# v's rows by plain fp32 products instead of split products and transposes, and eight new constants for the planner

## The chip, the cores and the metric

The kernel runs on one core of one Trainium2 chip. The metric is the device time of one execution in microseconds (us); the kernel before took 1351.64 us, the median of three executions (1351.54, 1351.64 and 1353.74 us). Five engines work side by side, each on its own instruction queue in order: TensorE (PE), VectorE (DVE), ScalarE (ACT), GpSimd (POOL) and SyncE (SP, which here only issues DMAs).

## The reference

The input x has 8 sequences of 512 rows and 128 channels, in fp32. Four residual blocks follow each other, each on the layer-normalised rows:

1. a Mamba-like block: input projection, depthwise convolution with silu, a scan over time with 8 states per channel, output projection;
2. a mixture of experts: 8 experts with hidden width 512, each `silu(x @ w_gate) * (x @ w_up)` and then `@ w_down`, weighted per row by a router;
3. attention with 16 heads of 8 channels, in which a row sees its own chunk of 10 rows and 25 rows to the left;
4. the same mixture of experts again.

In the attention block, `q = x @ Wq.T + bq`, and likewise k and v, where x is the normalised row. The scores are softmaxed under the mask and multiplied with v, and Wo follows. The change touches only how v is computed, and the constants of the planner.

## The kernel before

**The stream.** The experts are the spine of the program. For 2 passes of 8 sequences, 8 experts and 4 quarters of the hidden width there are three products on PE: g, u and y (128x128 weights against 512 columns). Each is a sum of three fp32r products, since weights and inputs are split into a high and a low part (`matmul3`, L489). Between them ACT computes silu(g), DVE multiplies by u, ACT or DVE rounds to the high part h0, and POOL subtracts to get the low part h1 (`hidden`, L1246). There are 2 x 8 x 8 x 4 = 512 such quarters. Only the first four experts of the first sequence are done in halves of 256 columns. The stream of a quarter needs a free PSUM bank for g, one for u, and h0 and h1 some quarters later for y.

**The side work.** Everything else (Mamba fronts and backs, router preparations, attention) is written as Python generators, "lanes", that yield the engine they need next. A planner written in the kernel (`Clock` L129, `Lanes` L280) keeps an own estimate of when each engine is free and decides, in Python and before the program is compiled, where in the stream's order each piece of side work goes. So the order of the instructions on each engine is fixed at build time; on the chip, semaphores alone decide when each starts. The planner's constants are at L94 to L120. The change touches these:

- `LATE` (L97, used at L1067): how early the router's exponentials may be placed when the wrong activation table is loaded;
- `SIDE` (L98) and `JOIN_MAX`, `JOIN_END` (L101, L103; `start`, L320): how long a side product that is ready waits so as to stand beside other side products;
- `WARM_GAP`, `WARM_TO` (L108, L109; `keep_warm`, L1763): where the planner expects PE to idle for longer than the gap, up to this place in the stream, it puts in a product whose result nobody uses (tile `idle`);
- `PRESS` and `HELD` (L111, L112; `tick`, L335): how much a late lane may push, and how long a lane is held back while the stream waits.

All instructions go through the wrapper at L269, so nearly every line of the profile says L269; groups are told apart by the names of tiles. Table loads of ACT that the kernel asks for itself are at L569.

**Attention's preparation.** `attention_consts` (L1328) runs once. `attention_prep` (L1341) runs once per sequence. It loads the rows, normalises them (`normalised`, L542; four PE transposes into `tp_a`, then high and low parts `axt`), and makes q and k by `matmul3` into `aqk`. Their pieces `apc` go to DRAM (`aqd`). Then, for v:

- three fp32r products of 512 columns give v transposed (`avp`); ACT adds the bias, one value per partition (`avf`);
- four PE transposes of 128x128 bring it back to rows (`avt`); ACT copies it to `avs`;
- one DMA of 256 KB writes `avs` to DRAM (`avd`), from where the attention's steps load windows of rows (`avr`).

`avf`, `avs` and the working tile `arest` of q and k share one buffer (tag "rest", one copy). The tile `xn` of a normalisation has one buffer too (`LNB = 1`), given back once its last reader is placed.

Of the kernel before, what the change touches and what calls it, by code (L numbers as in the profile page):

```python
# [8 lines left out]
F32 = mybir.dt.float32  # L9
# [3 lines left out]
AF = mybir.ActivationFunctionType  # L13
ALU = mybir.AluOpType
# [4 lines left out]
P = 128  # L19
B, L, DIM = 8, 512, 128  # L20
NT = L // P
# [47 lines left out]
B_BV = B_ROUTE + 32  # L69
# [24 lines left out]
AHEAD = 0.2  # L94
EDGE = 0.1
FIRST = 0.6
LATE = 0.3  # L97
SIDE = 0.5  # L98
JOIN = 2.0
JOIN_DUE = 0.0  # L100
JOIN_MAX = 6.0  # L101
JOIN_ATT = 3.0
JOIN_END = 2.0  # L103
MOST = 6
OTHERS = 4
AT_FIRST = 7
WARM = 3.5
WARM_GAP = 0.25  # L108
WARM_TO = 1.5  # L109
SECOND = 0.2  # L110
PRESS = 0.4  # L111
HELD = 0.18  # L112
MAMBA_DUE = 0.9
PREP_DUE = 0.9
ATT_LEAD = 2.5
# [164 lines left out]
class Lanes:  # L280
# [39 lines left out]
    def start(self, lane):  # L320
# [5 lines left out]
        if need == "T":  # L326
            if lane in self.urgent:
                return c.now if c.based("T", ready) <= c.now else INF
            wait = SIDE
            if not c.beside and not self.starved:  # L330
# [4 lines left out]
    def tick(self):  # L335
# [3 lines left out]
        while True:  # L339
            c.now = max(c.now, c.end["T"])  # L340
            first, best = c.now + AHEAD, None
            for lanes in (self.urgent, self.lanes):
                for lane in lanes:
# [3 lines left out]
                    else:  # L347
                        edge = PRESS if lane[4] and lane[4]() else 0.0
                        if self.starved:
                            edge = -HELD  # L350
                    if s <= c.now + max(AHEAD, edge) and s - edge < first:
# [26 lines left out]
def block_kernel(ctx: ExitStack, tc: tile.TileContext, x, pack_a, pack_b, pack_c, w_qkv, mask, mask_t, w_o,  # L378
# [3 lines left out]
    lanes = Lanes(clock)  # L382
    pe = Engine(nc.tensor, "T", clock)
    act = Engine(nc.scalar, "A", clock)
    dve = Engine(nc.vector, "V", clock)
    pool = Engine(nc.gpsimd, "P", clock)
    sp = Engine(nc.sync, "S", clock)

    const = ctx.enter_context(tc.tile_pool(name="const", bufs=1))
    dram = ctx.enter_context(tc.tile_pool(name="dram", bufs=1, space=DRAM))  # L390
    lnp = ctx.enter_context(tc.tile_pool(name="lnp", bufs=LNB))
    fp = ctx.enter_context(tc.tile_pool(name="fp", bufs=2))
    qp = ctx.enter_context(tc.tile_pool(name="qp", bufs=1))
# [32 lines left out]
    def sides(*tiles):  # L426
        while not bank("others", OTHERS if "first" in done else AT_FIRST, len(tiles)):
            yield lambda: bank("others", OTHERS if "first" in done else AT_FIRST, len(tiles))
        return take("others", *zip(*tiles))

    def side(shape, name):
        return (yield from sides((shape, name)))[0]

    def freed(t, who="others"):

        held[who] -= 1
        lanes.give("bank", t + TO_PE)
        return t
# [36 lines left out]
    pb = const.tile([P, B_COLS], F32, name="pb")  # L475

    ident = const.tile([P, P], F32, name="ident")
# [11 lines left out]
    def matmul3(dst, w, v, start=True, stop=True, after=0.0):  # L489

        clock.beside = False
        pe.matmul(dst, w[0], v[0], start=start, stop=False, after=after)
        pe.matmul(dst, w[1], v[0], start=False, stop=False)
        return pe.matmul(dst, w[0], v[1], start=False, stop=stop)
# [47 lines left out]
    def normalised(xc, tag, halves, nt=NT, give=True, quick=False, plain=False):  # L542


        yield "V", xc[1]
        xn = yield from layernorm(xc, tag, nt, quick)
        if give:
            lanes.give("x", max(clock.end["V"], clock.end["A"]))
        tp = yield from side([P, L], f"tp_{tag}")
        for t in range(nt):  # L550
            e = pe.transpose(tp[:, t * P : (t + 1) * P], xn[:, t, :], ident)
        if not plain:
            lanes.give("ln", e)
        yield "A"
        hi, lo = halves()
        tp = tp[:, : nt * P]
        e = act.copy(hi, tp)
        if plain:
            xn = xn.rearrange("p t d -> p (t d)")[:, : nt * P]
            e = act.copy(xn, tp)  # L560
        yield "V"
        freed(max(e, dve.tensor_tensor(lo, tp, hi.bitcast(F32), ALU.subtract)))
        yield "T"
        return (hi, lo, xn) if plain else (hi, lo)
# [458 lines left out]
    def ffn_prep(k, b, xc, t0=0, nt=NT):  # L1023
# [42 lines left out]

        yield lambda: clock.table in TABLES[AF.Exp] or pos[0] >= k * B + b - LATE  # L1067
        yield "A"
# [43 lines left out]
    def ffn_finish(k, b, acc):  # L1112
        xo, there = yield from load_x(b, 2 * k + 1, f"fo{k}_{b}")
        yield "T", there
        tp = yield from side([P, NT, DIM], f"yp{k}_{b}")
        for t in range(NT):
            pe.transpose(tp[:, t, :], acc[:, t * P : (t + 1) * P], ident)
        yield "V"
        freed(dve.tensor_tensor(xo, xo, tp, ALU.add))
        yield "S"  # L1120
        store_x(b, 2 * k + 2, xo)

    def ffn_stream():
# [14 lines left out]
        def weighted(k, b, e, cs, y, there):  # L1138
# [25 lines left out]
            elif left[0] == 0:  # L1164
                lanes.add(ffn_finish(k, b, state.pop(("acc", k, b))), rank=FRANK, ready=t, joins=JOIN_END)

# [161 lines left out]
    def attention_consts():  # L1328
        raw = qp.tile([P, 3, P], F32, tag="rest", name="wqkv")
        there = sp.dma_start(out=raw, in_=w_qkv) + 1.5  # L1330
        yield "A", there
        consts = []
        for i, nm in enumerate(("wq", "wk", "wv")):
            consts.append((yield from split_const(raw[:, i, :], P, nm)))
            yield "A"
        return consts

    scaling = HD ** -0.5
# [2 lines left out]
    def attention_prep(b, consts):  # L1341
        xc = yield from load_x(b, 2, f"a{b}")

        def halves():
            return [qp.tile([P, L], F32R, tag=f"t{i}", name=f"axt{b}_{i}") for i in range(2)]

        xt = yield from normalised(xc, f"a{b}", halves)
        stacks = []
        for m, (bcol, order) in enumerate(((B_BQ, Q_PIECES), (B_BK, K_PIECES))):
            pp = yield from side([P, L], f"aqk{b}_{m}")  # L1350
            matmul3(pp, consts[m], xt)
            yield "A"

            bias = pb[:, bcol : bcol + 1]

            qd = dram.tile([2, len(order), P // 2, L], BF16, tag=f"qd{m}", name=f"aqd{b}_{m}", bufs=2)

            def put(piece, pi):
                js = [j for j, o in enumerate(order) if o == pi]
                places = slice(js[0], js[-1] + 1, js[1] - js[0] if len(js) > 1 else 1)  # L1360
                for s in range(2):
                    half = piece[64 * s : 64 * s + 64, None, :]
                    sp.dma_start(
                        out=qd[s, places].rearrange("j r t -> r j t"),
                        in_=half.to_broadcast([64, len(js), L]),
                    )

            ps_ = [qp.tile([P, L], BF16, tag="pc", name=f"apc{b}_{m}_{i}", bufs=3) for i in range(3)]
            rest = qp.tile([P, L], F32, tag="rest", name=f"arest{b}_{m}")
            act.activation(ps_[0], pp, AF.Identity, bias=bias)  # L1370
            yield "V"
            freed(dve.scalar_tensor_tensor(rest, pp, bias, ps_[0], ALU.add, ALU.subtract))
            put(ps_[0], 0)
            yield "V"
            dve.tensor_copy(ps_[1], rest)
            yield "V"
            dve.tensor_tensor(ps_[2], rest, ps_[1], ALU.subtract)
            put(ps_[1], 1)
            yield "S"
            put(ps_[2], 2)  # L1380
            stacks.append(qd.rearrange("s j (d p) t -> s (j d) p t", p=NPAIR))
            yield "T"
        vp = yield from side([P, L], f"avp{b}")
        matmul3(vp, consts[2], xt)
        yield "A"
        vf = qp.tile([P, L], F32, tag="rest", name=f"avf{b}")
        freed(act.activation(vf, vp, AF.Identity, bias=pb[:, B_BV : B_BV + 1]))
        yield "T"
        vt = yield from side([P, NT, P], f"avt{b}")
        for t in range(NT):  # L1390
            pe.transpose(vt[:, t, :], vf[:, t * P : (t + 1) * P], ident)
        yield "A"
        vs = qp.tile([P, NT, P], F32, tag="rest", name=f"avs{b}")
        freed(act.copy(vs, vt))
        yield "S"
        vd = dram.tile([L, P], F32, tag="vd", name=f"avd{b}", bufs=2)
        e = sp.dma_start(out=vd.rearrange("(t p) d -> p t d", p=P), in_=vs)
        heads[b] = stacks[0], stacks[1], vd, e + 3.0

    def attention_preps():  # L1400
# [19 lines left out]
    def attention(sb):  # L1420
# [62 lines left out]
        def scores(s, both):  # L1483

            qs, ks, _ = loaded[s]
            for m in range(NPAIR):
                for h in range(2):
                    rows = slice(64 * h, 64 * h + QROWS)
                    for i, (q, k) in enumerate(blocks(steps[s][1])):
# [4 lines left out]
                        )  # L1494
            lanes.add(maxima(s, both, e), joins=JOIN_MAX)

# [101 lines left out]
        def outputs(s, o, e):  # L1598
# [11 lines left out]
            if t == len(QTILES) - 1:  # L1610
                lanes.add(joined(b, outs.pop(b)), rank=JRANK, ready=e, joins=JOIN_END)

# [103 lines left out]
    with mctx:  # L1716
# [28 lines left out]
        while (0, 0) not in ready or ready[0, 0][1] == 0:  # L1745
            if lanes.tick():
                continue
            if clock.now > WARM:
                sel = mc["sel"]
                e = pe.matmul(warm[:, :HALF], sel[:, 0], sel[:, : HALF // P], start=True, stop=True)  # L1750
# [12 lines left out]
        def keep_warm():  # L1763

            if pos[0] < WARM_TO and clock.now > clock.end["T"] + WARM_GAP and lanes.are_free("bank"):
                t, = take("experts", [[P, L]], ["idle"])
# [94 lines left out]
```

## Time and profile before

| what | value |
|---|---|
| median of three executions | 1351.64 us |
| the profiled execution | 1351.62 us |
| its span, first to last instruction | 1349.8 us |
| PE busy | 1328.9 us, 98% of the span |
| DVE, ACT, POOL busy | 1036.8, 964.7, 940.4 us |
| DMA queue for data, share of 16 engines | 33.9% |
| v's products `avp` (24 of them) and transposes `avt` (32) | 9.6 us and 5.1 us busy |
| ACT's `avf` and `avs`, one per sequence each | 686 and 586 ns median |
| mean granted clock of PE | 0.996 |

A time of PE's instructions is given in two ways. The duration of one matmul includes the latency through the array (393 ns for 512 columns), and the matmuls overlap; what counts for the end is the time from the start of one to the start of the next. In the timeline, that is the difference of the start times of two rows. "Idle before" names what an engine waited for.

### The profile page before, as it was taken

How to read it: one execution, taken by the hardware profiler on the slowest of the kernel's cores; microseconds unless marked ns; L12 is line 12 of the kernel's file. 1: busy time of each engine (PE TensorE's matmuls, PEld its weight loads, DVE VectorE, ACT ScalarE, POOL GpSimd, SP SyncE). 2: the span in 40 equal slices, each digit the busy share in tenths (PEclk: the TensorE clock that was granted, in tenths of full speed). 3: DMA queues.
4: the chain of work that ended last, by engine and by line, in shares of the span. 5: the costliest groups of instructions: out<-in, count | busy, mean ns of one | idle time of the engine just before them, and what ended most of it. 6: DMA issues, size and time to landing. Idle time of an engine off the chain costs nothing.

```text
span 1349.8 us, 29533 instructions
## 1 busy us (share of the span) xinstructions
PE 1328.9 (98%) x10261; PEld 1053.3 (78%) x10261; DVE 1036.8 (77%) x3114; ACT 964.7 (71%) x1694; POOL 940.4 (70%) x1042
## 2 busy tenths in 40 slices
PE   7999999999999999999999999999999999999998
PEld 7877778788788877777777777777777777778887
DVE  6887888688888867898788887888888787855443
ACT  7768576867787556777777777777877767765654
POOL 5877576776767757666766767767677676777776
PEclk9999999999999999999999999999999999999999
DMA  3321304232112242344345444454544434222111
GB/s 126 95 72 38 87 24 101 62 81 73 45 48 56 63 85 54 73 97 118 79 103 111 99 106 100 104 109 89 118 91 104 119 71 88 61 69 55 40 40 40
DMA packets 230861, 107.75 MB, mean 80 GB/s; under 512 B 86417, under 2 KB 226616, under 8 KB 230712
## 3 DMA queue, kind: packets, MB, share of 16 engines
q1 hardware_dynamic: 230712, 105.87, 33.9%
q8 instruction: 81, 1.33, 0.4%
q14 instruction: 68, 0.56, 0.1%
HBM read 77.64 MB, written 27.79 MB: 78 GB/s over the span
## 4 chain that ended last, share of the span: by engine, by line
PE 89%; POOL 3%; ACT 3%; issue 3%; DVE 2%; DMA 0%; POOLq 0%; DVEq 0%
PE u L269 25%; PE y L269 25%; PE g L269 25%; PE ao L269 2%; PE aw L269 2%; PE as L269 2%; POOL h L269 1%; PE mo L269 1%; PE aqk L269 1%; ACT h L269 1%; DVE h L269 1%; PE mde L269 1%; PE aout L269 1%; PE yp L269 1%; ACT L269 1%
## 5 line engine op out<-in xcount | busy, mean ns | idle before, releaser
L269 POOL TENSOR_TENSOR h<-h,h 128x512 fp32r<-128x512 f32 x492 | 640.0, 1310 | 279.0 <-ACT h L269 219.4
L269 PE MATMUL u<-xt_f,wu 128*128 128x512 f32 (+1 forms) x1584 | 451.5, 395 | 3.5 <-ACT h L269 2.7
L269 PE MATMUL g<-xt_f,wg 128*128 128x512 f32 (+1 forms) x1584 | 448.3, 393 | 2.1 <-ACT h L269 1.9
L269 PE MATMUL y<-h,wd 128*128 128x512 f32 (+1 forms) x1584 | 445.5, 392 | 1.4 <-POOL h L269 0.8
L269 DVE TENSOR_TENSOR h<-u,h 128x512 f32<-128x512 f32 x420 | 285.9, 686 | 157.5 <-PE u L269 109.3
L269 ACT ACTIVATE h<-g 128x512 f32<-128x512 f32 x512 | 303.4, 597 | 123.2 <-PE g L269 100.1
L269 ACT CAST h<-h 128x512 fp32r<-128x512 f32 x437 | 268.4, 619 | 171.2 <-DVE h L269 169.6
L269 PEld LDWEIGHTS g<-xt_f,wg 128*128 128x128 f32 x1584 | 288.5, 189 | 70.3 <-ACT h L269 3.0
L269 PEld LDWEIGHTS y<-h,wd 128*128 128x128 f32 x1584 | 288.3, 188 | 70.2 <-POOL h L269 1.4
L269 PEld LDWEIGHTS u<-xt_f,wu 128*128 128x128 f32 x1584 | 286.6, 189 | 71.7 <-ACT h L269 4.1
L269 POOL TENSOR_TENSOR acc<-acc,cwb 128x512 f32<-128x512 f32 (+1 forms) x114 | 148.0, 1298 | 52.5 <-DVE cwb L269 33.8
L269 ACT ACT_TABLE_LOAD x109 | 139.8, 1283 | 24.7 <-PE g L269 23.2
L269 DVE CUSTOM_DVE_ANT_0 amasked<-as,maskq 128x60 f32<-128x60 f32 x640 | 95.4, 213 | 5.0 <-PE as L269 4.8
L269 DVE TENSOR_TENSOR cwb<-y,cwb 128x512 f32<-128x512 f32 (+1 forms) x116 | 77.5, 668 | 16.0 <-PE y L269 14.4
L269 DVE TENSOR_TENSOR apt<-aw,maskk 125x400 f32<-125x400 f32 (+2 forms) x160 | 88.1, 570 | 0.0
L269 DVE SCALAR_TENSOR_TENSOR h<-h,g 128x512 f32<-128x512 f32 x92 | 62.3, 681 | 27.0 <-ACT h L269 26.6
L269 ACT ACTIVATE apt<-apt 125x400 f32<-125x400 f32 (+2 forms) x160 | 81.5, 540 | 0.4
L269 DVE SCALAR_TENSOR_TENSOR h<-u,h 128x512 f32<-128x512 f32 x92 | 62.6, 683 | 3.3 <-PE g L269 0.5
L269 DVE DVE_READ_ACCUMULATOR2_ANT amx<- 128x1 f32 x640 | 52.1, 81 | 0.0
L269 DVE CAST h<-h 128x512 fp32r<-128x512 f32 x75 | 48.8, 651 | 1.2
L269 DVE COPY v<-avr 125x128 f32<-125x128 f32 (+2 forms) x40 | 25.7, 644 | 26.4 <-PE ao L269 26.4
L269 PEld LDWEIGHTS ao<-apt,v 125*32 125x32 f32 (+2 forms) x1280 | 27.4, 109 | 14.6 <-DVE h L269 4.4
(205 smaller groups left out, 1239.5 us busy)
## 6 DMA issues: line engine op xcount, KB each, us to landing
cwb<-cwd_f SPq DMA_DIRECT2D x124, 256.0 KB
aqd<-apc SPq DMA_DIRECT2D x32, 192.0 KB
ks<-aqd SPq DMA_DIRECT2D x48, 93.8 KB
x_fo<-x SPq DMA_DIRECT2D x16, 256.0 KB
aqd<-apc SPq DMA_DIRECT2D x32, 128.0 KB
x_f<-x SPq DMA_DIRECT2D x15, 256.0 KB
qs<-aqd SPq DMA_DIRECT2D x48, 75.0 KB
aod<-aos SPq DMA_DIRECT2D x24, 100.0 KB
```

Of the source, the lines that this page charges most:

```text
L269: f(*args, **kw)
```

## The change

`attention_consts` no longer splits Wv into two parts; it copies it as plain fp32. It also makes a tile `bv` in which every partition holds v's bias along the columns: POOL spreads the bias column over a 128x128 tile (`bvs`), one PE product with the identity turns it (`abv`), and ACT copies it out.

`attention_prep` asks `normalised` for the plain fp32 copy of the transposed rows too (one more ACT copy out of PSUM, `xn_a` from `tp_a`), as the router's preparation does already. Right after the normalisation, v's rows come directly from four fp32 products: the stationary operand is a 128x128 slice of the transposed rows, and the moving one is Wv. DVE adds `bv` while it reads the result from PSUM into `avs`, and the DMA to `avd` follows. q and k come after that. The `xn` buffer of the normalisation is given back after v's products.

The eight constants above get new values, so the planner places the whole program anew.

```diff
-LATE = 0.3
-SIDE = 0.5
+LATE = 0.4
+SIDE = 0.6
-JOIN_MAX = 6.0
+JOIN_MAX = 8.0
-JOIN_END = 2.0
+JOIN_END = 5.0
-WARM_GAP = 0.25
-WARM_TO = 1.5
+WARM_GAP = 0.15
+WARM_TO = 2.5
-PRESS = 0.4
-HELD = 0.18
+PRESS = 0.3
+HELD = 0.1
...
-        for i, nm in enumerate(("wq", "wk", "wv")):
+        for i, nm in enumerate(("wq", "wk")):
             consts.append((yield from split_const(raw[:, i, :], P, nm)))
             yield "A"
+        wv = const.tile([P, P], F32, name="wv")
+        act.copy(wv, raw[:, 2, :])
+
+        wide = qp.tile([P, P], F32, tag="t0", name="bvs")
+        yield "P"
+        pool.tensor_copy(wide, pb[:, B_BV : B_BV + 1].to_broadcast([P, P]))
+        yield "T"
+        bp = yield from side([P, P], "abv")
+        pe.matmul(bp, wide, ident, start=True, stop=True)
+        bv = const.tile([P, P], F32, name="bv")
+        yield "A"
+        freed(act.copy(bv, bp))
+        consts += wv, bv
...
-        xt = yield from normalised(xc, f"a{b}", halves)
+        *xt, xf = yield from normalised(xc, f"a{b}", halves, plain=True)
+        vt = yield from side([P, NT, P], f"avt{b}")
+        for t in range(NT):
+            e = pe.matmul(vt[:, t, :], xf[:, t * P : (t + 1) * P], consts[2], start=True, stop=True)
+        lanes.give("ln", e)
+        yield "V"
+        vs = qp.tile([P, NT, P], F32, tag="rest", name=f"avs{b}")
+        freed(dve.tensor_tensor(vs, vt, consts[3][:, None, :].to_broadcast([P, NT, P]), ALU.add))
+        yield "S"
+        vd = dram.tile([L, P], F32, tag="vd", name=f"avd{b}", bufs=2)
+        v_end = sp.dma_start(out=vd.rearrange("(t p) d -> p t d", p=P), in_=vs)
+        yield "T"
...
-        vp = yield from side([P, L], f"avp{b}")
-        matmul3(vp, consts[2], xt)
-        yield "A"
-        vf = qp.tile([P, L], F32, tag="rest", name=f"avf{b}")
-        freed(act.activation(vf, vp, AF.Identity, bias=pb[:, B_BV : B_BV + 1]))
-        yield "T"
-        vt = yield from side([P, NT, P], f"avt{b}")
-        for t in range(NT):
-            pe.transpose(vt[:, t, :], vf[:, t * P : (t + 1) * P], ident)
-        yield "A"
-        vs = qp.tile([P, NT, P], F32, tag="rest", name=f"avs{b}")
-        freed(act.copy(vs, vt))
-        yield "S"
-        vd = dram.tile([L, P], F32, tag="vd", name=f"avd{b}", bufs=2)
-        e = sp.dma_start(out=vd.rearrange("(t p) d -> p t d", p=P), in_=vs)
```

More of the change, by code (lines that the diff above doesn't have):

```diff
@@ L1362, in put @@
                     half = piece[64 * s : 64 * s + 64, None, :]
-                    sp.dma_start(
+                    end = sp.dma_start(
                         out=qd[s, places].rearrange("j r t -> r j t"),
@@ L1366, in put @@
                     )
+                return end
             ps_ = [qp.tile([P, L], BF16, tag="pc", name=f"apc{b}_{m}_{i}", bufs=3) for i in range(3)]
@@ L1379, in attention_prep @@
             yield "S"
-            put(ps_[2], 2)
+            e = put(ps_[2], 2)
             stacks.append(qd.rearrange("s j (d p) t -> s (j d) p t", p=NPAIR))
             yield "T"
-        vp = yield from side([P, L], f"avp{b}")
-        matmul3(vp, consts[2], xt)
-        yield "A"
-        vf = qp.tile([P, L], F32, tag="rest", name=f"avf{b}")
-        freed(act.activation(vf, vp, AF.Identity, bias=pb[:, B_BV : B_BV + 1]))
-        yield "T"
-        vt = yield from side([P, NT, P], f"avt{b}")
-        for t in range(NT):
-            pe.transpose(vt[:, t, :], vf[:, t * P : (t + 1) * P], ident)
-        yield "A"
-        vs = qp.tile([P, NT, P], F32, tag="rest", name=f"avs{b}")
-        freed(act.copy(vs, vt))
-        yield "S"
-        vd = dram.tile([L, P], F32, tag="vd", name=f"avd{b}", bufs=2)
-        e = sp.dma_start(out=vd.rearrange("(t p) d -> p t d", p=P), in_=vs)
         heads[b] = stacks[0], stacks[1], vd, e + 3.0
```

## The prediction

> **What bounds the kernel now.** I read the page first (busy shares, clock, chain), then PE's list of waits, then PE's timeline around v's work and around each long wait, and ACT's timeline at one of them.
>
> ```profile
> PE 1328.9 (98%) x10261; PEld 1053.3 (78%) x10261; DVE 1036.8 (77%) x3114; ACT 964.7 (71%) x1694; POOL 940.4 (70%) x1042
> ...
> PE 89%; POOL 3%; ACT 3%; issue 3%; DVE 2%; DMA 0%; POOLq 0%; DVEq 0%
> ```
>
> PE is busy 98% of the span, and 89% of the chain that ended last is PE. So a microsecond of start-to-start time on PE is a microsecond of the whole, and work of other engines costs only where it makes PE wait. The next view is PE's timeline around v's work of one sequence (start, duration, instruction).
>
> ```profile
> 608.46 0.50 PE L269 MATMUL avp<-axt,wv_hi 128*128 128x512 f32 x1
> 608.80 0.40 PE L269 MATMUL avp<-axt,wv_lo 128*128 128x512 f32 x1
> 609.03 0.39 PE L269 MATMUL avp<-axt,wv_hi 128*128 128x512 f32 x1
> 609.26 0.86 PE L269 MATMUL y<-h,wd 128*128 128x512 f32 x3
> 609.96 0.86 PE L269 MATMUL g<-xt_f,wg 128*128 128x512 f32 x3
> ...
> 614.17 0.60 PE L269 MATMUL avt<-ident,avf 128*128 128x128 f32 x4
> 614.60 0.22 PE L269 MATMUL amt<-eye,mp 128*80 128x128 bf16 x1
> 614.63 0.94 PE L269 MATMUL g<-xt_f,wg 128*128 128x512 f32 x3
> 615.42 0.87 PE L269 MATMUL u<-xt_f,wu 128*128 128x512 f32 x3
> ```
>
> A stream triple takes 0.70 (609.26 to 609.96). The triple after a small product takes 0.79 (614.63 to 615.42): a switch of shape costs about 0.09. `avp` took 0.80 here, after the attention's `aw`; `avt` took 0.43. Plain fp32 products of the very shape that the change puts in exist already, in the attention's output `aout`:
>
> ```profile
> 1083.77 1.05 PE L269 MATMUL aout<-wo,aat_t 128*128 128x128 f32 x8
> 1084.58 0.95 PE L269 MATMUL g<-xt_f,wg 128*128 128x512 f32 x3
> ```
>
> Four such products take 0.81 between stream triples (eight rows, since an fp32 product runs in two), and 0.91 after `aw` (642.03 to 642.94 in the same view).
>
> PE's other time is waiting. I took each group on PE, start to start, against the median of groups with the same kind and neighbours. The medians sum to 1326.4; 17.9 us lie above them, 2.3 before the first and 3.2 after the last. Of the 17.9, the opening to 33 us holds 2.3, 59 to 92 us 5.9, 122 to 131 us 1.3, 148 to 153 us 1.3, 173 to 182 us 3.75, 262 to 267 us 1.7, 520 us 0.9; nearly nothing comes later. The largest place, on PE, on ACT, and its granted clock (third column from the right):
>
> ```profile
> 173.81 0.86 PE L269 MATMUL y<-h,wd 128*128 128x512 f32 x3
> 176.60 1.64 PE L269 MATMUL g<-xt_f,wg 128*128 128x512 f32 x3 [1.94 <-ACT h L269]
> 178.04 1.48 PE L269 MATMUL u<-xt_f,wu 128*128 128x512 f32 x3
> 179.32 1.19 PE L269 MATMUL y<-h,wd 128*128 128x512 f32 x3
> ...
> 169.68 1.28 ACT L569 ACT_TABLE_LOAD   x1
> 170.97 1.95 ACT L269 ACTIVATE mdec<-mdelta,nega 128x512 f32<-128x512 f32 x3
> ...
> 177.00:181.00 4.00, 4.00 (x18) 0.62 0.12 30
> ```
>
> ACT runs a Mamba batch between two table loads while silu(g) queues behind it; PE runs out of banks, waits 1.94, and then runs at a clock of 0.62 for three triples.
>
> **The change, part by part.**
>
> *v's products on PE.* Gone are 8 triples `avp` (5.76 start to start, all rows) and 8 times 4 `avt` (4.14): 9.9 us. In the changed order v's products stand between stream triples in four sequences, after `aw` in three, and before a small product in one: 4 x 0.81 + 3 x 0.91 + 0.9 = 6.9. Gain 3.0. The bounds per sequence are 0.81 and 1.09 (`aout` between two `aw`), so a gain of 1.2 to 3.4.
>
> *The bias tile.* `abv` is one 128x128 fp32 product, 0.22 by `mo` from `pa`, with a switch of 0.09: +0.3, once. POOL's `bvs` (about 0.2 by the small copies), ACT's copies of `wv` and `bv` (0.28 each, like `win`), less a rounding and a subtraction of the old split: beside the stream.
>
> *Shape switches.* From the order: 450 between the stream, the packed small products and single 128x128 products before, 455 after. By kind (five more back to the stream from single ones, five fewer from packed ones, at 0.08 and 0.10) that is nothing. One more `idle` product: 0.1. **PE's own work: -2.7**, as the same medians put over the changed order also give.
>
> *ACT, DVE, SP.* Per sequence ACT loses `avf` (0.69) and `avs` (0.59) and gains `xn_a` (0.58, as `axt`); DVE gains one add from PSUM (0.68 as `axt`). ACT is 71% and DVE 77% busy, and where PE does not wait the stream covers them: zero, unless they fall into a batch (below). SP's `avd` issue (0.37, 256 KB) now stands ahead of the twelve `aqd` issues of q and k; the readers come hundreds of microseconds later for the first sequences. The normalisation's only buffer is held for 5 to 9 us more per sequence; the order was made with that and places the next normalisation behind it. Cover: the preparations run a whole sequence ahead. If it is gone, the price is a wait like the one at 520 us, 0.9 each.
>
> *The planner's constants: where the waits go.* The first 203 PE instructions (to about 41 us) are the same, and so is the end from the last y of the second expert of the last sequence on. Between them I summed, per quarter of an expert, ACT's rows between two silus against PE's rows of that quarter, and carried on what ACT did not get done. This backlog, in us, against what PE lost:
>
> - before: 7.4 at 59 us (5.9 lost), 4.6 at 116 us (1.3), 5.7 at 167 us (3.75), 5.7 at 257 us (1.7); below 4 nothing.
> - changed order, same places in the stream: 7.0, then 6.2, then 5.1, then 4.1; elsewhere at most 4.2.
>
> So at the third place the batch is 1.2 shorter (the copies `xt_f` and `xn_f` stand elsewhere): the wait of 2.1 falls to about 1.0 and, like the wait of 1.45 at 265.42, should leave the clock alone: -2.7. The fourth goes: -1.7. The second grows by 1.6 of backlog: +1.0 (bounds 0 and 2.5, that of the third). In 59 to 92 us ACT has 0.4 less and 4 `idle` products stand instead of 10, but DVE's backlog by the same count peaks at 10.4 instead of 8.2 and stays 2 to 4 higher: +0.5 (bounds -3 and +3). For waits that appear where I see none: +1.3, one of the small kind (bounds 0 and 3.75). The places at 148 and 520 us: unchanged. Sum of waits: -1.6.
>
> On the price of a wait the Trainium skill ("TensorE: Matmul & The Clock Gate", section on HAM oscillation) gives another rule: no idle gaps on PE above about 3.4 us. By it a 1.94 us gap costs only itself; the rows above show 1.65 more at a clock of 0.62. By the rule the third place would give back 1.1 instead of 2.7, and the sum would be 1348.9.
>
> **Sum.** -2.7 - 1.6 = -4.3. The profiled execution took 1351.62 (span 1349.8 and 1.8 around it), the same as the median 1351.64: **1347.3 us**.
>
> **Rivals.**
>
> *The waits only move.* The batches are the same in number (124 table loads for 125), and a place with less ACT backlog gets more of DVE. For it: DVE's higher count at 64 to 92 us. Against: the two shorter batches. Then the waits stay at 17.9 and PE's own gain is left: 1348.9, or, with the opening at its bound of +3, 1351.9.
>
> *A new wait in DVE's queue (slower).* `avs` and `arest` share one buffer. q's first `arest` on DVE must now wait until the DMA has read `avs`. From add to free buffer: issue 0.4 plus about 3.0 (the first load of 256 KB, 0.72 to 3.8 us) is 3.4, and 6.9 where SP stands behind another wait (3.3 to 3.5 us late in two of eight rows). From v's products to q's the changed order has 5.2 to 8.5 us of PE. Behind `arest` in DVE's queue stand the stream's multiplications by u, for which first ACT and POOL and then y wait. DVE carried a backlog of 6.7 at 138 us without loss to PE. So it decides only where SP is late and DVE is also several microseconds behind: from three sequences on, at 2.1 to 3.75 each, -4.3 + 3 x 2.9 = +4.4: 1356.
>
> *All late waits vanish.* Then -2.7 and the 9.0 after 92 us go: 1340. For it: every backlog after the second place is below 5.2. Against: the second place's 6.2.
>
> *The change doesn't do what it says.* Were v's fp32 products as dear as in the dearest row, 1.09 each, PE's gain would shrink by 1.8: 1349.1.
>
> **How the numbers follow.** Forecast 0.45 (own range 1344.5 to 1349.5), waits only move 0.25 (with the dear products), new DVE wait or a worse opening 0.18, late waits vanish 0.12. The range: 1341.5 to 1354.5 leaves out about half of each outer case. A measurement of this kernel tells about 0.2% (2.7 us) from no change, so faster means below 1348.9 and slower above 1354.3. Faster: 0.12, nine tenths of the forecast and a quarter of the second case, about 0.6; slower: most of the third, 0.15; the rest same.
>
> **What would show it.** `avp` is gone and `avt` takes 0.81 to 0.92 to the next start. PE's busy sum falls by about 3 us. At the batch near 165 us (third place) PE's idle is about 1 and the clock stays at 1.00; nothing is lost near 255 us; something like 2 us is lost near 120 us. Wrong would be: idle time before stream triples after 270 us released by DVE h, with `arest` waiting for the DMA of `avs`; or 59 to 92 us losing 9 or more.

## The result and the profile after

The changed kernel takes 1362.54 us (median of six executions, 1359.8 to 1365.54); the kernel before, on the same chip, 1351.59. The ratio is 1.0082, with a 95% interval of 1.0063 to 1.0101: **slower by 11 us**, where 1347.3 was forecast, with 1341.5 to 1354.5 as the range. The profiled execution of the changed kernel took 1365.54 us, with a span of 1363.8 (before: 1349.8).

The page of the changed kernel, busy times (first line) and the chain that ended last by engine (second line):

```profile
PE 1333.6 (98%) x10272; PEld 1056.0 (77%) x10272; DVE 1033.2 (76%) x3098; ACT 957.5 (70%) x1707; POOL 936.4 (69%) x1043
...
PE 82%; ACT 4%; DVE 4%; POOL 3%; DMA 3%; issue 2%; SPq 1%; POOLq 0%; ACTq 0%; DVEq 0%
```

PE's share of the chain fell from 89 to 82%, and DMA, which had 0%, has 3%. PE's busy sum rose, from 1328.9 to 1333.6, although it issues less work: a triple of the stream behind a wait is busy for up to 1.48 us instead of 0.86 (below). So I did again what the prediction did for the kernel before: each group on PE, start to start, against the median of before for its kind and neighbours.

- **PE's own work** (the sum of the medians of before over the groups of the order): 1326.4 before, 1322.9 after: -3.4 (forecast: -2.7). v's eight groups `avt` alone, taken as measured from start to start, sum to 6.9 us (forecast: 6.9).
- **What lies above the medians** (waits, and the slow clock behind them): 17.9 before, 35.3 after: +17.4 (forecast: -1.6).

Both together are the 14.0 us between the spans. Up to 300 us the excess is 16.0 before and 14.7 after (forecast: 13.4, which is 16.25 + 0.5 + 1.0 - 2.7 - 1.7); beyond 300 us it is 1.9 before and **20.6** after. The loss lies where the prediction had seen next to nothing.

The waits of DVE, without those on PE, ACT and POOL, show what is new. The columns are the engine and the tile that waited, what it waited for, us in total, times, the longest. Before:

```profile
DVE aover L269 <- DMA aover<-aod: 1.3, 2, 0.8
...
DVE cwb L269 <- DMA cwb<-cwd_f: 0.5, 2, 0.4
```

After:

```profile
DVE aover L269 <- DMA aover<-aod: 9.8, 4, 4.7
...
DVE acc L269 <- DMA cwb<-cwd_f: 6.4, 4, 2.2
...
DVE cwb L269 <- DMA cwb<-cwd_f: 4.5, 3, 3.3
...
DVE aat_t L269 <- DMA aall_over<-aoverd: 3.6, 1, 3.6
```

`aover` holds attention's softmax sums of a sequence, which come back from DRAM and are inverted on DVE; `aall_over` is their inverse, spread over the partitions; `cwb` holds the router's weights of one expert. In all 24.3 us against 1.8. The largest place is at 628 us. The chain of waits there (start, duration, what; SPq is SP issuing a DMA):

```profile
623.00 0.05 issue
623.05 0.67 SPq L269
623.73 0.05 issue
623.78 5.95 DMA aover<-aod
629.73 0.03 issue
629.75 0.02 DVEq L269
629.77 0.04 issue
629.82 0.55 DVE aover L269
...
631.45 0.14 issue
631.58 0.99 PE ao L269 x32
```

DVE had finished everything ahead of `aover` in its queue at 625.13 and stood for 4.69 us. The same operation on DVE, in the kernel before (first line) and after (second line):

```profile
618.83 0.55 DVE L269 RECIPROCAL aover<-aover 128x64 f32<-128x64 f32 x1
...
629.82 0.55 DVE L269 RECIPROCAL aover<-aover 128x64 f32<-128x64 f32 x1 [4.69 <-DMA aover<-aod]
```

Behind `aover` stood the row maxima (`amasked`, `amx`), with which the next attention products are made. On PE, in the timeline:

```profile
628.34 0.86 PE L269 MATMUL y<-h,wd 128*128 128x512 f32 x3
631.58 0.96 PE L269 MATMUL ao<-apt,v 110*32 110x110 f32 x32 [2.38 <-DVE amx L269]
...
634.49 1.63 PE L269 MATMUL g<-xt_f,wg 128*128 128x512 f32 x3
635.92 1.48 PE L269 MATMUL u<-xt_f,wu 128*128 128x512 f32 x3
637.20 1.48 PE L269 MATMUL y<-h,wd 128*128 128x512 f32 x3
```

PE waits 2.38, and then a triple takes 1.28 from start to start instead of 0.70 (635.92 to 637.20); the granted clock is 0.50 from 634.5 to 638.5 us. The groups between 625 and 650 us lose 5.9 us for this one late DMA. At 810 us the same happens with `cwb`: its issue at 806.45 stands on the chain behind six others of 0.57 to 0.87 us in a row, it takes 5.68 to land, `acc` on DVE waits for it, PE waits 2.14, and the clock is 0.55 from 813 to 816.7. The DMA on the chain, then the wait on PE:

```profile
806.45 5.68 DMA cwb<-cwd_f
...
812.90 1.30 PE L269 MATMUL g<-xt_f,wg 128*128 128x512 f32 x3 [2.14 <-DVE acc L269]
```

So the kernel computes v as forecast and at the forecast price. At these two places, which hold 10.0 of the 20.6 us, and at two smaller ones (1.5 us where DVE waits 3.56 for `aall_over` at 920 us, 1.3 us where it waits 2.38 for `aover` at 1153 us), the planner's order puts a reader of a DMA so early into DVE's in-order queue that the DMA has not landed. Not all of the loss is of this kind: near 340 us (2.1 us) the chain runs over POOL, ACT and DVE and holds no DMA, and from 479 to 486 us (2.2 us) DVE waits 2.82 for POOL and then 2.10 for `cwb`. The planner counts 0.55 us for an issue and 1.4 plus the bytes for the landing (`Clock.run`).

### The profile page after: what moved, and what is told of

Its sections match the earlier page's. It is cut to its first block, busy times and chain, and to the rows that moved or that the text cites. A ratio compares the mean times of both kernels' runs of the same rounds, so it can differ in the third digit from the quotient of the medians.

```text
span 1363.8 us, 29535 instructions
## 1 busy us (share of the span) xinstructions
PE 1333.6 (98%) x10272; PEld 1056.0 (77%) x10272; DVE 1033.2 (76%) x3098; ACT 957.5 (70%) x1707; POOL 936.4 (69%) x1043
## 4 chain that ended last, share of the span: by engine, by line
PE 82%; ACT 4%; DVE 4%; POOL 3%; DMA 3%; issue 2%; SPq 1%; POOLq 0%; ACTq 0%; DVEq 0%
PE u L269 23%; PE y L269 23%; PE g L269 23%; PE ao L269 2%; PE aw L269 2%; ACT h L269 2%; PE as L269 2%; POOL h L269 1%; DVE h L269 1%; SPq L269 1%; PE mo L269 1%; DMA cwb<-cwd_f 1%; ACT L269 1%; PE aqk L269 1%; PE yp L269 1%
## 5 line engine op out<-in xcount | busy, mean ns | idle before, releaser
L269 DVE CAST h<-h 128x512 fp32r<-128x512 f32 x75 | 45.6, 614 | 1.1
L269 PE MATMUL ao<-apt,v 125*32 125x100 f32 (+2 forms) x1280 | 36.4, 254 | 2.4 <-DVE amx L269 2.4
```

What stands on the lines that cost most here:

```text
L269: f(*args, **kw)
```

## The experiments

**Theory A**: PE's price of v is as predicted; the loss comes from the order alone. A newly planned order draws waits of its own, in the changed kernel those on DMAs above; the order before happens to be nearly free of them. **The rival**: v's new code or one of the new constants is itself dear.

**Each half of the change alone.** v's new code with the old constants, and the old code with the new constants.

```
-LATE = 0.4
-SIDE = 0.6
+LATE = 0.3
+SIDE = 0.5
...
-PRESS = 0.3
-HELD = 0.1
+PRESS = 0.4
+HELD = 0.18
```

```
-        *xt, xf = yield from normalised(xc, f"a{b}", halves, plain=True)
+        xt = yield from normalised(xc, f"a{b}", halves)
...
+        vp = yield from side([P, L], f"avp{b}")
+        matmul3(vp, consts[2], xt)
...
```

> The changed code of v with the eight constants of before. The changed kernel loses 19.8 us on PE after 300 us, the kernel before about 1. Theory A (DVE, in its queue, waits for DMAs that the planner placed too early behind SP's bursts, and each new order draws its own such waits): PE's own rows sum to 1321.0 in this order, 5.4 less than before; the time is 1346 plus whatever waits for DMAs this order has, and DVE's waits for aover and cwb account for what lies above 1347. Theory B (v's new code makes the waits, by its earlier DMA and its held buffers): 1358 to 1363. Theory C (the new constants make them): 1345 to 1348.

> The code of v as before with the eight new constants. PE's own rows sum to 1325.5, 0.9 less than before. Theory A: between 1350 and 1365, and what lies above 1351 is found again as DVE's waits for DMAs. Theory B: 1350 to 1352. Theory C: 1361 to 1366, the loss of the changed kernel plus its 2.7 us of PE work.

Measured: 1360.58 us, ratio 1.0056 (1.0038 to 1.0074), for the new code alone; 1358.3 us, 1.0034 (1.0021 to 1.0047), for the new constants alone. Both halves are slower by themselves, and each has waits of its own on DVE: the first waits for `cwb` (9.2 us on five occasions), the second for `aover` (5.2) and `apc` (2.5). The first time alone would also fit theory B (1358 to 1363); the second (B: 1350 to 1352, C: 1361 to 1366) fits A alone. The first also has the wait of the prediction's second rival: `arest` stands 2.8 us until the DMA has read `avs`. The new code alone has the lowest own work on PE (1321.0) and an excess of 34.4; the new constants alone have work of 1325.5 and an excess of 22.8.

**One constant put back.** JOIN_END, alone.

```
-JOIN_END = 5.0
+JOIN_END = 2.0
```

> The changed kernel with the one constant JOIN_END (how long an end of a sequence waits to stand beside other side products) back at 2.0. PE's own rows sum to 1323.3, 0.4 more than in the changed kernel. Theory C with this constant as the culprit, since the losses lie where ends of the attention and the experts meet: 1350 to 1353. Theory A: no constant is the culprit; the order after the first end is another one and draws other waits, 1350 to 1365.

Measured: 1365.57 us, 1.0093 (1.0069 to 1.0117). The place near 630 us is there again (DVE waits 4.47 for `aover`, PE 2.16), and so are those for `cwb` and `acc` at 464 and 484 us; later the waits are others, among them `arest` with 4.3 for the DMA of `avs`. It is not this constant.

**One wait taken away in the same order.** The reciprocal reads a constant instead of the sums, so that DVE has no reason to wait for their DMA; the kernel leaves out the division by the sums, and everything else keeps its place.

```
-dve.reciprocal(over, over)
+dve.reciprocal(ones, half_power[:, :1].to_broadcast([P, L // HD]))
-e = sp.dma_start(out=overd..., in_=over)
+e = sp.dma_start(out=overd..., in_=ones)
```

> The changed kernel in the same order, but the reciprocal of the softmax's sums reads a constant instead of the loaded sums, and its result goes on; so the DMA of the sums is still issued, and DVE doesn't wait for it. It leaves out the division by the sums. Theory A: DVE waited 9.8 us in four places for these sums; PE lost 5.9 us at the largest one near 628 us, which goes, and the rest of the loss (cwb, all_over) stays: 1355 to 1358. If DVE's wait for the sums is only where another limit shows (PE's banks, ACT), the time stays within 2 us of the changed kernel.

Measured: 1361.12 us, 1.0054 (1.0023 to 1.0086). The place at 628 us is gone. PE's timeline there:

```profile
626.59 0.68 PE L269 MATMUL as<-ks,qs 48*32 48x60 bf16 x64
627.20 0.43 PE L269 MATMUL aw<-qs,ks 51*125 51x100 bf16 x8
627.56 0.97 PE L269 MATMUL u<-xt_f,wu 128*128 128x512 f32 x3
628.37 0.86 PE L269 MATMUL y<-h,wd 128*128 128x512 f32 x3
```

Nothing waits, and the triples keep their 0.70. Beyond 300 us the excess falls from 20.6 to 12.9: without the waits for the sums 7.7 us of the loss are gone, in these two profiles. `cwb` (6.0), `acc` (5.8) and `aat_t` (3.3) still wait. The times show less: the gain is 1.4 us in the medians, 3.8 us by the two ratios to before (the two kernels were timed on different chips), and the intervals overlap. The 1355 to 1358 us of theory A were missed, and by the time alone the other outcome of its text (within 2 us of the changed kernel) stands. Up to 300 us this profile has 3.3 us more than that of the changed kernel, in the same order. So the place itself is settled by the trace; its share of the whole loss is not settled by the times.

**The kernel before, nudged.** If an order draws its waits, then one that differs from before for no reason at all must draw some too.

```
-SIDE = 0.5      -PRESS = 0.4
+SIDE = 0.51     +PRESS = 0.41
```

> The kernel before with one constant of the planner nudged, SIDE 0.51 for 0.5: no work is added or taken away, only the order from about 165 us on differs (439 shape switches on PE for 450; PE's own rows, by the medians of the trace before, sum to 1325.6 us for 1326.4). Theory A (every other order draws its own waits of DVE and PE on DMAs that the planner takes for landed; the order before is nearly free of them): 1354 to 1362 us, with DVE waiting 5 to 20 us in all for aover, cwb or the like, where before shows 1.3. Rival (the loss comes from v's new code or from the new constants themselves): 1350 to 1353 us, and these waits below 3 us.

> The kernel before with another constant nudged, PRESS 0.41 for 0.4: the order differs from about 70 us on (453 shape switches for 450; PE's own rows 1325.4 us for 1326.4). Theory A: again 1354 to 1362 us, with waits at other places than in the first nudged order. Rival: 1350 to 1353 us. One of the two nudged orders near 1352 and the other above 1356 would say that the draw is wide, and speaks for A too.

Measured: SIDE 0.51 gives 1355.23 us, 1.0019 (1.0009 to 1.0029); PRESS 0.41 gives **1365.91**, 1.0097 (1.0079 to 1.0116), as slow as the changed kernel. Neither adds or removes work. So a constant moved by 2.5% can cost 13 us. Both expectations were met in part only: SIDE lies in the forecast 1354 to 1362, but it is only 2.2 us above the 1353.07 of before on that chip, and DVE waits 4.5 us for `aover` and `cwb`, where 5 to 20 for these or the like were forecast; PRESS is above the forecast. One part of the theory falls here: in the order of PRESS 0.41 DVE waits only 4.7 us for `aover` and 3.5 for `cwb`. Most of its losses are batches on ACT instead (beyond 300 us PE waits 8.4 us for ACT's `h`), the kind that the prediction had costed up to 300 us. ACT in the timeline, then PE:

```profile
394.16 1.28 ACT L569 ACT_TABLE_LOAD   x1
395.45 1.95 ACT L269 ACTIVATE mdec<-mdelta,nega 128x512 f32<-128x512 f32 x3
397.44 0.72 ACT L269 ACTIVATE mdelta<-mdelta,nega 128x512 f32<-128x512 f32 x1
398.07 0.61 ACT L269 CAST h<-h 128x512 fp32r<-128x512 f32 x1
398.58 0.87 ACT L269 ACTIVATE xn_f<-x_f,nm_f,rs_f 128x128 f32<-128x128 f32 x2
399.47 1.28 ACT L269 ACT_TABLE_LOAD   x1
```

```profile
401.41 1.33 PE L269 MATMUL u<-xt_f,wu 128*128 128x512 f32 x3 [2.71 <-ACT h L269]
```

A Mamba batch, a rounding and a normalisation lie between two table loads, and silu(g) comes after the second: PE waits 2.71. So theory A holds in its wider form only: what a new order draws may be a wait for a DMA or a batch on ACT.

**The planner told that DMAs land later.** The readers of `aover`, `aall_over` and `cwb` are planned 3 us later; no work changes.

```
 def weighted(...):
-            yield "V", max(there, come)
+            yield "V", max(there, come + 3.0 * (pos[0] > 1.0))
 def joined(...):
-            yield "V", e
+            yield "V", e + 3.0
-            yield "PV", max(e, at_there)
+            yield "PV", max(e, at_there) + 3.0
```

> v's new code with the old constants, and the same 3 us told to the planner (PE's own rows 1321.3 us; 1321.0 without the 3 us). Theory A: DVE's waits for cwb and acc, 12.3 us without the margin, fall below 5 us, and the time from 1360.6 to 1348 to 1356 us. Rival: no change against 1360.6 us.

> The changed kernel, in which the planner is told that the DMAs of the softmax sums, of the weighted values and of the windows before them land 3 us later than it thought, so that it places their readers on DVE later; the work itself is the same (PE's own rows 1321.6 us by the medians of before, 1322.9 in the changed kernel). Theory A: DVE's waits for aover, cwb and all_over fall from about 18 to below 6 us, and the time to 1348 to 1356 us. Rival (these waits cost nothing, or the loss is the products' own): 1360 us or more. New waits elsewhere of 5 us or more with those of DVE gone would say that the loss only moves with the order.

> The kernel before, in which the planner is told that the DMAs of the softmax sums, of the weighted values and of the windows before them land 3 us later (PE's own rows 1325.2 us for 1326.4). With v's new code and the old constants the same 3 us brought 1360.6 down to 1353.2. If the margin is a cure in general, this gives 1346 to 1351 us. Theory A in its wider form (a new order draws new waits of whatever kind, and the order before is already one of the good ones): 1352 to 1364 us, with DVE's waits for aover and cwb below 2 us all the same.

In all three the waits fall as expected: DVE waits 0.4 us for `cwb` with the new code and the old constants, 1.0 for `cwb` and 1.0 for `aover` in the changed kernel, none for either in the kernel before. The times do not follow them. Theory A gave 1348 to 1356 us for the first two, and 1352 to 1364 in its wider form for the third. The new code with the old constants gains 7.4 us, to 1353.24, 0.9996 (0.9987 to 1.0006). The changed kernel gets *slower*, 1374.44, 1.016 (1.014 to 1.0181); the kernel before too, 1356.09, 1.0024 (1.0014 to 1.0033). So the forecast was missed for the changed kernel, by 18 us. The margin removes its waits, but it is also a new order. What the changed kernel drew with it contains the very wait of the prediction's second rival. Its DVE in the timeline:

```profile
1040.62 0.69 DVE L269 SCALAR_TENSOR_TENSOR h<-h,g 128x512 f32<-128x512 f32 x1 [1.00 <-ACT h L269]
1043.44 0.75 DVE L269 SCALAR_TENSOR_TENSOR arest<-aqk,pb,apc 128x512 f32<-128x512 f32 x1 [2.14 <-DMA avd<-avs]
...
1058.24 0.36 DVE L269 BATCH_NORM_AGGREGATE mv_f<-st_f 128x2 f32<-128x6 f32 x4
```

And its PE:

```profile
1052.93 0.41 PE L269 MATMUL aw<-qs,ks 51*110 51x110 bf16 x8
1061.13 0.48 PE L269 MATMUL tp_f<-ident,xn_f 128*128 128x128 f32 x1 [7.80 <-ACT xn_f L269]
```

`arest` waits 2.14 us until the DMA has read `avs` out of the shared buffer. Then DVE works through its queue without a pause up to 1058.6, where the statistics of a normalisation stand last; `tp_f` needs that normalisation and is already next on PE, which waits 7.80. The 2.14 are not the whole of it: how much of the 7.80 is their part and how much the normalisation placed too early was not separated.

**The change without a new order.** The decisive test keeps the kernel's order: the planner is still told the old operations' costs, and the new ones are issued at their places (`planned` adds an operation to the planner's clock and issues nothing; what is issued directly on the engine, `nc.`, the planner does not see). In the full version DVE adds up the two parts of the rows and then v's bias, in place of ACT's `avf` and `avs`. v stays behind q and k, as in the kernel before, so this tests the fp32 products, not the place that the changed kernel gives them.

```
-matmul3(vp, consts[2], xt)
+for i, j in ((0, 0), (1, 0), (0, 1)):
+    pe.planned("matmul", vp, consts[1][i], xt[j])
+nc.vector.tensor_tensor(xf, xt[0].bitcast(F32), xt[1].bitcast(F32), ALU.add)
...
-pe.transpose(vt[:, t, :], vf[:, t * P : (t + 1) * P], ident)
+nc.tensor.matmul(vt[:, t, :], xf[:, t * P : (t + 1) * P], wv, start=True, stop=True)
+pe.planned("transpose", vt[:, t, :], xf[:, t * P : (t + 1) * P], ident)
...
-freed(act.copy(vs, vt))
+nc.vector.tensor_tensor(vs, vt, bv[:, None, :].to_broadcast([P, NT, P]), ALU.add)
+freed(act.planned("copy", vs, vt))
```

> v's rows by plain fp32 products in exactly the order of the kernel before: the planner is still told the old operations' costs (3 products, ACT's bias, 4 transposes), so that every other instruction of PE, ACT, DVE, POOL and SP stands where it stood. PE issues 4 products at the place of the 4 transposes and nothing at that of avp; avf on ACT is gone. Left out: v's bias and the low part of the rows (the products read the high part of axt). Theory A (the products are worth what the prediction said, the loss comes from the new order alone): PE's own work falls by 3.0 us and no wait comes, so 3.0 us below before: a ratio of 0.9978, DVE's waits for DMAs as in before (1.3 us). Rival (the products are dearer than their rows, or any change of the times along a fixed order brings waits too): a ratio of 1.000 or more.

> As order_kept_pe, but nothing is left out: DVE adds the high and the low part of the rows (0.60 us per sequence) and v's bias (0.68 us) at places that the planner knows nothing of, in place of ACT's avf and avs (0.69 and 0.59); one product abv and its copies come once (0.3 us). PE's own work falls by 2.7 us. Theory A: 0 to 2.7 us below before, a ratio of 0.998 to 1.000, since 1.28 us more for DVE in eight places is hidden or costs a few tenths each; this would be the version that is not slower than either. Rival: DVE's additions are late for PE's products by about 1 us each and the time is 1.003 or more.

Measured, in five rounds each: 1351.06 us, 0.9990 (0.9980 to 0.9999), for the products alone, and **1350.97 us, 0.9989 (0.9980 to 0.9997)**, for the full version: 1.7 and 1.8 us below the 1352.74 of before on that chip. In the profiles the spans are 1348.6 and 1348.2, PE's own work 1323.2 and 1323.4 (before: 1326.4), and beyond 300 us the excess is 4.3 and 4.1 (before: 1.9). DVE's waits for `aover` and `cwb` are 2.4 and 3.1 us in all. Theory A had 3.0 us less for the products alone, a ratio of 0.9978 and no new wait; the gain is smaller, and a little waiting did come (`as` on PE waits 1.25 us for the DMA of `ks` at 489 us). For the full version it had 0 to 2.7 us less, and that holds. PE and then DVE of the full version, at the sequence that the prediction showed:

```profile
612.77 0.86 PE L269 MATMUL y<-h,wd 128*128 128x512 f32 x3
613.46 1.05 PE L1416 MATMUL avt<-wv,avf 128*128 128x128 f32 x8
614.35 0.22 PE L269 MATMUL amt<-eye,mp 128*80 128x128 bf16 x1
614.38 0.95 PE L269 MATMUL g<-xt_f,wg 128*128 128x512 f32 x3
```

```profile
609.12 0.72 DVE L1410 TENSOR_TENSOR avf<-axt,axt 128x512 f32<-128x512 f32 x1
615.01 0.68 DVE L1420 TENSOR_TENSOR avs<-avt,bv 128x512 f32<-128x512 f32 x1
```

The four products take 0.89 from start to start, where `avp` and `avt` took 0.80 and 0.43. In all, v's groups on PE take 7.2 us from start to start in these two versions, where `avp` and `avt` took 9.9 before. The change is worth about 3 us on PE, a little over half of it reaches the end (0.4 to 2.7 us by the interval), and DVE's 1.28 us more per sequence cost nothing that can be seen beside the version without them. This is the one complete version that beats both kernels. What the changed kernel's other novelties cost by themselves (v ahead of q and k, the longer held buffer of the normalisation, ACT's copy `xn_a`) is not separated from the new order by any run.

All orders side by side, in us, from one profile each but for the last column:

| order | PE's own work | excess to 300 us | beyond | span | ratio to before |
|---|---|---|---|---|---|
| before | 1326.4 | 16.0 | 1.9 | 1349.8 | 1 |
| order kept, v's new products | 1323.4 | 15.2 | 4.1 | 1348.2 | 0.9989 |
| new code, old constants, 3 us margin | 1321.3 | 18.3 | 6.6 | 1351.7 | 0.9996 |
| before, SIDE 0.51 | 1325.6 | 15.8 | 7.0 | 1353.9 | 1.0019 |
| before, 3 us margin | 1325.2 | 16.6 | 7.0 | 1354.3 | 1.0024 |
| old code, new constants | 1325.5 | 12.0 | 10.8 | 1353.8 | 1.0034 |
| new code, old constants | 1321.0 | 20.3 | 14.1 | 1361.0 | 1.0056 |
| the changed kernel | 1322.9 | 14.7 | 20.6 | 1363.8 | 1.0082 |
| changed, JOIN_END 2 | 1323.3 | 14.0 | 18.9 | 1361.8 | 1.0093 |
| before, PRESS 0.41 | 1325.4 | 15.7 | 16.3 | 1363.0 | 1.0097 |
| changed, 3 us margin | 1321.6 | 15.9 | 32.9 | 1376.0 | 1.0160 |

PE's own work spans 5.4 us over these orders, the excess beyond 300 us spans 31. In the main it is the latter that sorts the ratios; a few neighbours change places. The order before has the least of it.

## Why the prediction was wrong

*v's products on PE*: right. Forecast 9.9 us gone and 6.9 come; in the changed kernel 6.9 came, 0.81 to 0.91 each, inside the bounds of 0.81 and 1.09. With the order kept 7.2 came. The parts of PE's own work in the forecast sum to -2.6, not -2.7, which changes nothing.

*The planner's constants, the places up to 300 us*: near in the sum (14.7 for 13.4), which is luck, since the parts are wrong both ways. The opening to 33 us, called the same, had 4.5 for 2.3. 59 to 92 us: 5.0 where 6.4 was forecast. 116 to 131 us: 0.7 for 2.3. Third place: the loss fell from 3.77 to 2.46, but not for the reason given. The wait was to shrink from 2.1 to 1.0 with the batch; its own row shows 1.94 before, and it is 1.93 after, so only the slow clock behind it is missing. That clock is no property of the order (last section). Fourth place: 0.9 for 0.

***"For waits that appear where I see none: +1.3, one of the small kind (bounds 0 and 3.75)"***: this is the step that failed. Measured: about 18.7 (20.6 against 1.9). The bound was the dearest place of the kernel before, as if an unseen wait came once; beyond 300 us at least six stretches of 25 us lose over 1 us each, the dearest 5.9. What made it look small was the backlog of ACT and DVE: it counts what an engine still has to do, and it was at most 4.2 in the changed order beyond 300 us. A reader that waits for a transfer has no backlog; the engine is idle. The trace of before could not price this, since there DVE waits 1.8 us in all for these DMAs. That is what a good order looks like, and it was taken for what any order looks like. The nudged orders show the same step failing where no work changed: 7.0 and 16.3 us beyond 300 us, for the 1.9 of before.

*ACT, DVE, SP at zero*: right for DVE's addition, as far as the full version with its order kept shows it (DVE has 1.28 us more per sequence there); ACT's copy `xn_a` was not tested alone. For SP it was too little to ask who reads `avd`: what matters is which transfers stand behind a burst of issues in its queue, as `cwb` does at 806 us.

*A new wait in DVE's queue (slower)*: the right engine, the right mechanism (an in-order queue that stands on a DMA) and the right side, with another DMA. In the changed kernel `arest` never waits for `avs`; it does for 2.8 to 4.3 us in three other orders with the new code. The price of 2.1 to 3.75 per place was too low for the two dearest (5.9 and 4.1).

*The waits only move* and *all late waits vanish*: neither. The forecast treated the new order as the old one with some terms corrected. Two nudged orders of the same work differ by 10.7 us, more than twice the forecast gain of 4.3.

## What to carry to other kernels

When a change makes a planner lay out a tuned program anew, forecast the new order as a draw from such orders, and not as the old order with corrections: here eight newly planned orders of the same or less work were 0.2 to 1.6% slower and one was equal, against 0.2% gained on PE and 0.1% in the time where the order was kept. To learn what an edit is worth in itself, and to keep it, hold the order fixed and tell the planner the old costs. In the trace, count the readers of transfers in the in-order queues and what SP issues just ahead of them, not only busy time and backlog.

## What the runs showed of the hardware

**After the same wait the clock fell in some profiles and stayed in others.** The batch on ACT near 175 us gives the same wait on PE, 1.93 to 1.96 us, in eleven of the thirteen profiles. In five of them (the kernel before among them) the triples behind it take up to 1.45 us from start to start; in six the clock stays. The prediction shows the place in the kernel before, with the next triple 1.44 us later (176.60 to 178.04); with the order kept it is 0.80:

```profile
176.73 0.97 PE L269 MATMUL g<-xt_f,wg 128*128 128x512 f32 x3 [1.96 <-ACT h L269]
177.53 0.86 PE L269 MATMUL u<-xt_f,wu 128*128 128x512 f32 x3
```

From 177 to 181 us the granted clock is 0.62 in the first, and from 176 to 180 us it is 1.00 in the second. The changed kernel and the run without the wait for the sums have the same order too: the clock is 1.00 behind this wait in the one (179.6 to 183.6 us) and 0.59 in the other (181.4 to 185.4 us). So the prediction's 1.65 us for the slow clock was the outcome of one execution; by five in eleven, about half of it is my estimate of a fair price. A wait of 2.31 us kept its clock too (PRESS 0.41, at 267 us), and two of 2.14 and 2.38 did not (above). The Trainium skill ("TensorE: Matmul & The Clock Gate", Part 1) says that the activity monitor looks at a window of about 3.4 us that runs freely and does not start anew with the kernel. The same wait with both outcomes agrees with that; no run here shows the window itself. Its section on HAM oscillation gives the rule of no gaps above about 3.4 us. These rows differ: five gaps of 1.93 or 1.94 us were followed by a slow clock, and six of 1.93 to 1.96 were not.

**A transfer of 16 KB can take 6 us from issue to landing.** `aover` is loaded in two issues of 16 KB, and in the changed kernel the second took 5.95 us from 623.78, while SP issued eight others for other tiles from 622.44 to 630.5. In the kernel before, DVE could start on the same tile at 618.83, 2.9 us after the first of the two issues (615.9). Whether the other issues made the difference was not tested.
